# An LSTM with a feed-forward network: the input products of the last 24 steps as seven products of quarters, and the gates in two pairs

## The chip, the core and the metric

The kernel runs on one core of a Trainium2 chip. The time is that of one launch on the device, in microseconds (us). PE is the matrix engine, ACT the scalar engine, DVE the vector engine, POOL the general-purpose engine, SP the engine that only issues transfers (DMAs). Each engine takes its instructions in program order and waits on semaphores for the others. The time before is 312.69 us, the median of three runs (312.64 to 312.83).

## What is computed

```python
def lstm_forward(x, h0, Wx, Wh, b):            # x (32, 64, 256), h0 = cond (32, 256)
    xW = jnp.einsum('ntd,dg->ntg', x, Wx) + b  # g: 4 * 256 columns, gates i, f, o, g
    def step(carry, xw_t):
        a = xw_t + prev_h @ Wh
        i, f, o = sigmoid of the first three gates of a;  g = tanh of the fourth
        next_c = f * prev_c + i * g
        next_h = o * jnp.tanh(next_c)
...
h = s0 * dense(k0, concatenate([h, -h]));  h = relu(h) * 2    # weights are +1 or -1 by bool
h = s1 * dense(k1, h);  h = relu(h) * 2                       # 1024 x 1024
h = s2 * dense(k2, h)
out = x + h
```

There are 64 dependent steps on a batch of 32, then three dense layers over all 2048 rows.

## The kernel before

**Layout.** A gate of 256 columns is spread over four groups of 32 partitions (q = 0 to 3), so that one step's batch of 32 fills 128 partitions with 64 columns for each gate. A product with 32 columns of stationary operand uses a quarter of the array's columns, and the kernel issues four of them side by side, one for each q. Such four matmuls are called a pass here. `x_part` (line 242) makes one pass of x Wx for a step `t` and half `k` of the 256 inputs: all four gates (256 moving columns), or two gates (128 columns), which is half a pass. A matmul of f32 stands in the trace as two instructions.

**Recurrence.** `gates_from_h` (line 301) adds h Wh to two PSUM banks: the first bank holds the gates g, i, f (192 columns), the second o (64 columns); the order in memory is `GATES = (3, 0, 1, 2)`. `cell_step` (line 319) applies on ACT sigmoid to i and f, tanh to g, sigmoid to o; DVE makes `kept`, `new` and `c`; ACT makes `th` = tanh(c); DVE makes `h` and turns it into `hist`, the next stationary operand. Last, ACT copies x Wx + b of the next step into the two gate banks (`gates_from_x`, lines 316 and 317).

**Order.** The order is written out by hand: each engine runs what the main loop (line 702) emits, in that order. A step emits the gates and the cell first, then filler work for PE, then chores for DVE and ACT. In the first `X_STEPS` = 21 steps the filler is x Wx of later steps (`x_products`, line 272); in the other 43 it is the dense layers of blocks of 16 steps (`ffn_block`, line 585), 576 matmuls of 512 columns in all. The filler is dealt out evenly by a running `goal`: 208 half passes over 21 steps are nine or ten for each step. The last block of 16 steps follows after the loop (`last_block`).

**Chores in the first stretch.** DVE adds the bias to each full bank of x Wx (`evict_x`, line 258, two steps' worth of 512 columns), turns blocks of x (`turn_x`, line 226, by `next_x`, which also issues the load of x two blocks on, on SP), makes parts of the weights `w0` (line 206) and the low half of h (`split_h`, line 344: ACT rounds `hist` to `hhi`, DVE forms the rest `hlo`; the dense layers read both). ACT also makes `w0t` (line 205) and one 1024-column row of `w1` in a step (line 211). A counter `load` of DVE chores in the step holds further chores back from two on; a split that has waited long enough is emitted in any case.

**Start.** PE first runs two matmuls that clear the gate banks and eight idle ones (`WARM_UP`). Wx arrives in six transfers, issued by SP and ACT. The products of the first eight steps are made in three sweeps: input half 0 with the slots 1 and 2, input half 0 with the slots 0 and 3, then input half 1 with all gates. Between the last two come the bias products. POOL issues the small transfers, makes some single-column constants, and then has nothing to do.

Of the kernel before, what the change touches and what calls it, by code (L numbers as in the profile page):

```python
# [30 lines left out]
F32 = mybir.dt.float32  # L33
# [8 lines left out]
def lstm_ffn(ctx: ExitStack, tc: tile.TileContext, x, cond, wx_d, wh_d, b_d, k0_d, k1_d, k2_d, s0_d, s1_d, s2_d, out):  # L42
    nc = tc.nc
# [13 lines left out]

    GATES = (3, 0, 1, 2)

    AHEAD = 12  # L60
    X_STEPS = 21

    FIRST_CHORE = 2
    W2_STEP = 24
    WARM_UP = 8

# [15 lines left out]
    def act(shape, dtype, name):  # L82
        return apool.tile(shape, dtype, tag="act", name=name)
# [33 lines left out]

    def load_gates(t, w_d, slots, engines, chunks=slice(0, 2)):

        w_rows = w_d.rearrange("(p b) g -> p b g", b=2)  # L120
        s0, n, g0 = slots[0], len(slots), GATES[slots[0]]
        if len(engines) == 1:
            halves = [slice(0, P)]
        else:
            halves = [slice(0, P // 2), slice(P // 2, P)]
        for engine, half in zip(engines, halves):
            engine.dma_start(
                out=t[half, chunks, s0 * H : (s0 + n) * H], in_=w_rows[half, chunks, g0 * H : (g0 + n) * H]
            )


    both = [nc.sync, nc.scalar]
    load_x(0, 0, both)
    for k in range(2):
        load_gates(wx, wx_d, (1, 2), [nc.sync], slice(k, k + 1))
        for slot in (0, 3):
            load_gates(wx, wx_d, (slot,), [nc.scalar], slice(k, k + 1))
    load_x(0, 1, both)
    load_gates(wh, wh_d, (1, 2), both)
    load_gates(wh, wh_d, (0,), [nc.scalar])  # L140
    load_gates(wh, wh_d, (3,), [nc.sync])

# [3 lines left out]
    b_rows = b_d.rearrange("(o g h) -> o g h", o=1, g=4)  # L146
    nc.gpsimd.dma_start(out=b_row[0][:1, :1], in_=b_rows[:, 3:])
    nc.gpsimd.dma_start(out=b_row[0][:1, 1:], in_=b_rows[:, :1])
    nc.gpsimd.dma_start(out=b_row[1][:1], in_=b_rows[:, 1:3])
    scales = []  # L150
# [58 lines left out]

    def make_w1(k):  # L210
        nc.scalar.activation(w1[:, k, :], bits[k], AF.Identity, bias=nsgn[1], scale=sgn2[1])  # L211
        load_bits(4 + k)

# [22 lines left out]

    load = [0]

# [19 lines left out]
    def evict_x(p, t):  # L258
        xg[t] = gpool.tile([P, 2, 4 * HQ], F32, tag="xg", name=f"xg{t}")
        b = bias.rearrange("p g j -> p (g j)").unsqueeze(1).to_broadcast([P, 2, 4 * HQ])  # L260
        load[0] += 1
        nc.vector.tensor_tensor(xg[t], p.rearrange("p t g j -> p t (g j)"), b, ALU.add)  # L262

    def next_x(half):

        if half < 2 * NB:
            load[0] += 1
            turn_x(*divmod(half, 2))
            if half + 4 < 2 * NB:
                load_x(*divmod(half + 4, 2), [nc.sync])  # L270

    def x_products(t0, t1):

        for t in range(t0, t1, 2):
            p = x_bank(t)
            for s in range(2):
                for k in range(2):
                    start = s == 0 and k == 0
                    passes = min(left_over[0], 2)
                    if passes == 1:  # L280
                        x_part(p, t + s, k, slice(0, 2), start)
                        yield 1
                        x_part(p, t + s, k, slice(2, 4), False)
                    else:
                        x_part(p, t + s, k, slice(0, 4), start)
                    if s == 1 and k == 1:
                        evict_x(p, t)
                        half, left = divmod(t + 2, SB // 2)
                        if left == 2 and half + 1 < 2 * NB:
                            turns.append(half + 1)  # L290
                        if left == 6 and turns:
                            next_x(turns.popleft())
                    yield passes


    hist, hparts = {}, {}

    gate_banks = [ps_g.tile([P, TB], F32, tag=f"gates{n}", name=f"gates{n}") for n in (3, 1)]
    gates = [g[:, : n * HQ].rearrange("p (g j) -> p g j", j=HQ) for g, n in zip(gate_banks, (3, 1))]

    def gates_from_h(t, hT):
        for g, slots in zip(gates, (slice(0, 3), slice(3, 4))):
            for k in range(2):
                for q in range(NQ):
                    nc.tensor.matmul(  # L305
                        g[q * N : (q + 1) * N],
                        hT[:, k, :],
                        wh_q[:, k, q, slots],
                        start=False,
                        stop=(k == 1),  # L310
                        skip_group_check=True,
                    )

    def gates_from_x(t):
        x_t = xg[t // 2 * 2][:, t % 2].rearrange("p (g j) -> p g j", g=4)
        nc.scalar.copy(gates[0], x_t[:, :3])  # L316
        nc.scalar.copy(gates[1], x_t[:, 3:])  # L317

    def cell_step(t, c):
        sig = cell.tile([P, 3, HQ], F32, tag="sig", name=f"sig{t}")  # L320
        cand = cell.tile([P, HQ], F32, tag="cand", name=f"cand{t}")
        nc.scalar.activation(sig[:, 0:2, :], gates[0][:, 1:3], AF.Sigmoid)  # L322
        nc.scalar.activation(cand, gates[0][:, 0], AF.Tanh)  # L323
        nc.scalar.activation(sig[:, 2, :], gates[1][:, 0], AF.Sigmoid)  # L324
# [33 lines left out]
    def evict(p, name):  # L358
        hi, lo = (act([P, TB], F32R, f"{name}{s}") for s in "hl")
        load[0] += 1  # L360
        nc.scalar.activation(hi, p, AF.Relu)
        nc.vector.scalar_tensor_tensor(lo, p, 0.0, hi, ALU.max, ALU.subtract)  # L362
        return hi, lo
# [276 lines left out]
    for g in gate_banks:  # L640
        nc.tensor.matmul(g, idle[:, :P], idle, start=True, stop=True)  # L641
    for n in range(WARM_UP):
        nc.tensor.matmul(p_idle, idle[:, :P], idle, start=True, stop=True)  # L643
# [10 lines left out]
    def copy_bias():  # L654
        p_bias = ps_o.tile([P, 4, HQ], F32, tag="po", name="p_bias")
        for q in range(NQ):
            for i, t in enumerate(b_row):
                nc.tensor.matmul(  # L658
                    p_bias[q * N : (q + 1) * N, 2 * i : 2 * i + 2],
                    first,  # L660
                    t.rearrange("p g (q j) -> p q g j", q=NQ)[:, q],
                    start=(i == 0),
                    stop=True,
                    skip_group_check=True,
                )
        nc.vector.tensor_copy(bias, p_bias)

    banks = [x_bank(t) for t in range(0, SB // 2, 2)]
    for slots in (slice(1, 3), slice(0, 4, 3)):
        for t in range(SB // 2):  # L670
            x_part(banks[t // 2], t, 0, slots, t % 2 == 0 and slots.start == 1)
    copy_bias()
    for t in range(SB // 2):
        x_part(banks[t // 2], t, 1, slice(0, 4), False)
        if t % 2:
            evict_x(banks[t // 2], t - 1)
            if t == 1:
                turn_x(0, 1)
# [13 lines left out]
    chores += [lambda k=k, h=h: make_w0(k, h) for k in range(2) for h in range(2)]  # L692
    chores += [lambda k=k: make_w1(k) for k in range(FC0)]
    chores2 = deque(lambda k=k, m=m: make_w2(k, m) for k in range(2) for m in range(2))
    sum_parts = deque(lambda s=s, k=k: make_sum(s, k) for k in range(K2) for s in range(1, 5))
    splits, w0_parts = deque(), deque()

    work = x_products(AHEAD, T)
    total_x = (T - AHEAD) * 4
    total_ffn = (NB - 1) * (4 * FC0 + 2 * FC0 * FC1 + 4 * FC1)  # L700
    done = 0
    for t in range(T):
        load[0] = 0
        gates_from_h(t, hT)
# [3 lines left out]
        if outputs:  # L708
            load[0] += 1
            if next(outputs[0], "end") == "end":  # L710
                outputs.popleft()
        if t == X_STEPS:
            work, done = ffn(), 0
        goal = (t + 1) * total_x // X_STEPS if t < X_STEPS else (t + 1 - X_STEPS) * total_ffn // (T - X_STEPS)
        while done < goal:
            left_over[0] = goal - done
            done += next(work)
        if t == X_STEPS - 1:
            next(work, None)

        if turns and load[0] < 2:
            next_x(turns.popleft())
        if splits and (load[0] < 2 or t >= X_STEPS or t == SH * splits[0] + 2 * SH - 1):
            split_h(splits.popleft())
        else:
            if t >= FIRST_CHORE and chores:
                part = chores.popleft()()
                if part is not None:
                    w0_parts.append(part)
            elif t >= W2_STEP and chores2:  # L730
                chores2.popleft()()
            if w0_parts and (load[0] < 2 or t == X_STEPS - 1):
                w0_parts.popleft()()
            if sum_parts and t >= SUM_STEP and load[0] < 2:
                sum_parts.popleft()()
    assert not sum_parts
# [31 lines left out]
```

## Time and profile before

| what | value |
|---|---|
| median of three runs | 312.69 us |
| the profiled execution, its own time | 312.31 us |
| its span, first to last instruction | 310.5 us |
| start, to the first gates | 16.60 us |
| first stretch, 21 steps | 63.4 us, a step mostly 3.03 us |
| second stretch, 43 steps | 183.4 us, a step 4.18 or 4.41 us |
| after the loop | 47.1 us |
| busy in the first stretch, of 63.40 us | PE 63.40, DVE 45.62, ACT 37.71, POOL 0.00 us |
| busy in the second, of 183.40 us | PE 183.28, DVE 96.51, ACT 80.70, POOL 0.00 us |
| granted PE clock | 1.00 in all stretches of the loop |

The last rows come from a table of busy time by stretch. A matmul's busy time runs until its result is written, so matmuls overlap in it, and a busy PE is not yet one at its peak; start-to-start times tell more. Busy time on the other engines is plain.

### The profile page before, as it was taken

The numbers are of one execution on the slowest core, as the hardware profiler recorded it, in microseconds if no ns is written. First come the engines' busy times: TensorE is split into PE (matmuls) and PEld (weight loads), VectorE is DVE, ScalarE is ACT, GpSimd is POOL, SyncE is SP. The second block draws the span as 40 slices with busy tenths as digits, with TensorE's granted clock in tenths as the row PEclk, the third lists the DMA queues.
The fourth block names the chain that finished last, engine by engine and source line by source line (L and its number), as shares of the span: only waits on it lengthen the run. The fifth ranks groups of instructions, "written<-read, shape, count | busy, mean of one in ns | idle before, by whom it ended". The sixth has DMA issues, their size and how long they took to land.

```text
span 310.5 us, 9798 instructions
## 1 busy us (share of the span) xinstructions
PE 304.5 (98%) x4138; PEld 242.7 (78%) x4138; DVE 178.1 (57%) x530; ACT 142.0 (46%) x512; POOL 6.6 (2%) x24
## 2 busy tenths in 40 slices
PE   8999999999999999999999999999999999999994
PEld 4888888788777777777777777777777777899993
DVE  2566767777673444355754445567554434698543
ACT  0225566774564543435633434355443333886220
POOL 5300000000000000000000000000000000000000
PEclk9999999999999999999999999999999999999999
DMA  6874001142000000000010000000310000131002
GB/s 192 206 196 99 5 19 38 36 95 65 3 2 0 2 2 0 3 2 0 2 38 22 14 3 0 2 2 13 92 34 2 3 0 2 31 79 27 2 0 69
DMA packets 30587, 10.89 MB, mean 35 GB/s; under 512 B 27720, under 2 KB 29768, under 8 KB 30544
## 3 DMA queue, kind: packets, MB, share of 16 engines
q1 hardware_dynamic: 27136, 8.66, 11.2%
q10 hardware_dynamic: 3168, 1.57, 2.0%
q8 instruction: 32, 0.52, 0.7%
q0 software_dynamic: 240, 0.04, 0.1%
q14 instruction: 11, 0.09, 0.1%
HBM read 8.16 MB, written 2.10 MB: 33 GB/s over the span
## 4 chain that ended last, share of the span: by engine, by line
PE 97%; DVE 1%; ACT 0%; issue 0%; ACTq 0%
PE p L617 30%; PE gates L305 20%; PE px L246 18%; PE p L591 8%; PE po L604 7%; PE gates L452 4%; PE po L561 2%; PE r L452 2%; PE x L452 2%; PE p L479 2%; PE p_idle L643 1%; PE gates L641 0%; DVE a_7l L362 0%; DVE o L388 0%; PE p_bias L658 0%
## 5 line engine op out<-in xcount | busy, mean ns | idle before, releaser
L305 PEld LDWEIGHTS gates<-wh,hist 128*32 128x32 f32 x2016 | 54.6, 109 | 22.3 <-issue 13.4
L305 PE MATMUL gates<-wh,hist 128*32 128x192 f32 x2016 | 68.1, 275 | 0.0
L246 PE MATMUL px<-wx,xT 128*32 128x256 f32 (+1 forms) x1168 | 60.5, 353 | 0.1
L322 ACT ACTIVATE sig<-gates 128x128 f32<-128x128 f32 x64 | 17.7, 277 | 80.6 <-PE gates L305 80.4
L246 PEld LDWEIGHTS px<-wx,xT 128*32 128x32 f32 x1168 | 42.4, 110 | 11.3 <-DVE c_first L652 0.7
L326 DVE TENSOR_TENSOR kept<-sig,c 128x64 f32<-128x64 f32 x63 | 14.2, 225 | 50.0 <-ACT sig L322 49.7
L332 ACT ACTIVATE th<-c 128x64 f32<-128x64 f32 x64 | 16.4, 257 | 31.4 <-DVE c L330 31.4
L334 DVE TENSOR_TENSOR h<-sig,th 128x64 f32<-128x64 f32 x64 | 14.4, 225 | 20.7 <-ACT th L332 20.7
L262 DVE TENSOR_TENSOR xg<-px,bias 128x512 f32<-128x512 f32 x32 | 21.2, 671 | 2.8 <-PE px L246 2.3
L316 ACT COPY gates<-xg 128x192 f32<-128x192 f32 x64 | 20.0, 313 | 1.3 <-DVE xg L262 1.3
L591 PE MATMUL p<-hhi,w 128*128 128x512 f32 x48 | 19.3, 402 | 0.0
L591 PE MATMUL p<-hlo,w 128*128 128x512 f32 x48 | 19.1, 398 | 0.0
L339 DVE STREAM_TRANSPOSE hist<-h 128x64 f32<-128x64 f32 x64 | 15.7, 245 | 2.4
L330 DVE TENSOR_TENSOR c<-kept,new 128x64 f32<-128x64 f32 x64 | 14.4, 224 | 2.2
L324 ACT ACTIVATE sig<-gates 128x64 f32<-128x64 f32 x64 | 14.9, 233 | 0.1
L323 ACT ACTIVATE cand<-gates 128x64 f32<-128x64 f32 x64 | 14.0, 218 | 0.0
L328 DVE TENSOR_TENSOR new<-sig,cand 128x64 f32<-128x64 f32 x64 | 13.9, 217 | 0.0
L317 ACT COPY gates<-xg 128x64 f32<-128x64 f32 x64 | 13.0, 203 | 0.0
L591 PEld LDWEIGHTS p<-hhi,w 128*128 128x128 f32 x48 | 9.0, 188 | 2.2
L591 PEld LDWEIGHTS p<-hlo,w 128*128 128x128 f32 x48 | 9.0, 188 | 2.0
L211 ACT ACTIVATE w<-bits,nsgn,sgn 128x1024 fp32r<-128x1024 uint8 x8 | 9.9, 1241 | 0.0
L617 PE MATMUL p<-a_7h,w 128*128 128x512 f32 x24 | 9.9, 413 | 0.0
(249 smaller groups left out, 602.8 us busy)
## 6 DMA issues: line engine op xcount, KB each, us to landing
x<-in_x_dram SPq DMA_DIRECT2D x60, 64.0 KB, 2.8
out_dram<-o SPq DMA_DIRECT2D x28, 64.0 KB, 1.8
bits<-in_L_ffn_k_dram SPq DMA_DIRECT2D x10, 128.0 KB, 3.2
wx<-in_L_cond_Wx_dram SPq DMA_DIRECT2D x2, 256.0 KB, 4.2
wx<-in_L_cond_Wx_dram ACTq DMA_DIRECT2D x4, 128.0 KB, 4.6
wh<-in_L_cond_Wh_dram ACTq DMA_DIRECT2D x2, 256.0 KB, 5.6
wh<-in_L_cond_Wh_dram SPq DMA_DIRECT2D x2, 256.0 KB, 6.2
k<-in_L_ffn_k_dram SPq DMA_DIRECT2D x2, 256.0 KB, 3.1
```

The source lines that it names most:

```text
L246: nc.tensor.matmul(p[q * N : (q + 1) * N, t % 2, slots], xT[i // 2, i % 2][:, s, k, :], wx_q[:, k, q, slots], start=start, stop=False, ski ...
L262: nc.vector.tensor_tensor(xg[t], p.rearrange("p t g j -> p t (g j)"), b, ALU.add)
L305: nc.tensor.matmul(g[q * N : (q + 1) * N], hT[:, k, :], wh_q[:, k, q, slots], start=False, stop=(k == 1), skip_group_check=True,)
L316: nc.scalar.copy(gates[0], x_t[:, :3])
L322: nc.scalar.activation(sig[:, 0:2, :], gates[0][:, 1:3], AF.Sigmoid)
L324: nc.scalar.activation(sig[:, 2, :], gates[1][:, 0], AF.Sigmoid)
L332: nc.scalar.activation(th, c, AF.Tanh)
L339: nc.vector.transpose(hT, h.rearrange("p (j b) -> p b j", b=2))
L452: nc.tensor.matmul(bank[pair][:, i], a(k)[:, ts(2 * pair + i, P)], b(k, n), start=first and i == 0 and k == 0 and n == 0, stop=last and k ...
L591: nc.tensor.matmul(p, w0[:, k, ts(m, P)], a[:, k, :], start=(n == 0), stop=(n == 3))
L604: nc.tensor.matmul(po[m], w2[:, m, k], a1[k][n], start=(k == 0 and n == 0), stop=(k == FC1 - 1 and n == 1))
L617: nc.tensor.matmul(p1[m], w1[:, k, ts(m, P)], a0[k][n], start=(k == 0 and n == 0), stop=(k == FC0 - 1 and n == 1),)
```

## The change

The x Wx of the steps 40 to 63 (eight-step halves of blocks, numbers 5, 6 and 7) is no longer made step by step. For each such half the product is a 2 x 2 block product: the inputs in two halves, the steps in two groups of four, the gates in two pairs (i, f) and (o, g). Instead of eight block products seven are made, on sums and differences: four sums of blocks of Wx on POOL (`sum_wx`, once), four differences of blocks of x on DVE for each half (`differ_x`), and copies and sums of the results by ACT and DVE. Each of the seven has four half passes. The gates stand in memory as i, f, o, g, the two gate banks hold a pair each (128 columns each), Wx arrives in five transfers and in another order, and the bias in two. `make_w1` makes half a row at a time; chores of ACT are counted in `copies`, those of DVE in columns (`load`, up to `ROOM`). Two of the idle matmuls now clear two banks for the quarters. The first stretch has 20 steps.

```diff
-    X_STEPS = 21
+    X_STEPS = 20
+    TURN_STEPS = (5, 9, 13)
+    BEGIN_STEPS = (8, 12, 15)
+    FIRST_QUARTERS = 5
+    QUARTERS = [
+        [(5, 1), (5, 7)], [(5, 2), (5, 6)], [(5, 5), (6, 1)], [(5, 3), (5, 4)], [(6, 7), (6, 6)], [(6, 2), (6, 5)],
+        [(7, 1), (6, 3)], [(6, 4), (7, 7)], [(7, 6), (7, 2)], [(7, 5)], [(7, 3), (7, 4)],
+    ]
-    WARM_UP = 8
+    WARM_UP = 6
...
+    for gates, k, engine in (
+        (slice(0, 2), 0, nc.sync), (slice(2, 3), 0, nc.scalar), (slice(3, 4), 0, nc.sync),
+        (slice(0, 2), 1, nc.scalar), (slice(2, 4), 1, nc.sync),
+    ):
+        load_gates(wx, wx_d, gates, [engine], slice(k, k + 1))
...
+    def sum_wx():
+        a11, a12 = wx[:, 0, : 2 * H], wx[:, 1, : 2 * H]
+        a21, a22 = wx[:, 0, 2 * H :], wx[:, 1, 2 * H :]
+        for i in (1, 2, 3, 4):
+            t = wx_sum[i] = act([P, 2 * H], F32, f"sx{i}")
...
+            nc.gpsimd.tensor_tensor(t, in0, in1, op)
+    def differ_x(i, ns):
...
+        load[0] += 360
+        for n in ns:
+            in0, in1 = {1: (b12, b11), 2: (b22, t[:, 0]), 3: (b22, b12), 4: (b21, t[:, 1])}[n]
+            nc.vector.tensor_tensor(t[:, n - 1], in0, in1, ALU.subtract)
+    def take_x(i, pair, half, p, other):
...
+        load[0] += 512
+        nc.vector.tensor_tensor(flat(t), flat(p), other, ALU.add)
+    def begin_r(i):
+        r = quarter_bank(ps_f, "pf", f"qr{i}")
...
+        nc.scalar.copy(flat(r), bias_of(1))
+    def x_products_of(i, n):
...
+        p = {1: x, 2: x, 7: r, 4: r}.get(n, q)
+        for s in range(SB // 4):
+            for k in range(NQ):
+                nc.tensor.matmul(
+                    p[k * N : (k + 1) * N, s],
+                    b[:, s],
+                    w[:, k],
...
+        if n == 1:
+            q = banks["q"] = quarter_bank(ps_o, "po", f"qq{i}")
...
+            nc.scalar.copy(q, x)
+        elif n == 2:
+            take_x(i, 0, 0, x, bias_of(0))
+        elif n in (6, 5):
+            t = uv[i, n] = act([P, SB // 4, 2, HQ], F32, f"uv{i}_{n}")
...
+            nc.scalar.copy(t, q)
+            if n == 5:
+                take_x(i, 1, 1, r, flat(t))
+        elif n == 3:
+            take_x(i, 0, 1, q, bias_of(0))
+        elif n == 4:
+            take_x(i, 1, 0, r, flat(uv[i, 6]))
...
-        nc.scalar.activation(sig[:, 0:2, :], gates[0][:, 1:3], AF.Sigmoid)
-        nc.scalar.activation(cand, gates[0][:, 0], AF.Tanh)
+        nc.scalar.activation(sig[:, 0:2, :], gates[0], AF.Sigmoid)
+        nc.scalar.activation(cand, gates[1][:, 1], AF.Tanh)
         nc.scalar.activation(sig[:, 2, :], gates[1][:, 0], AF.Sigmoid)
...
+        if t in TURN_STEPS:
+            turns.append(FIRST_QUARTERS + TURN_STEPS.index(t))
+        if t in BEGIN_STEPS:
+            begin_r(FIRST_QUARTERS + BEGIN_STEPS.index(t))
+        if X_STEPS - len(QUARTERS) <= t < X_STEPS:
+            for i, n in QUARTERS[t - X_STEPS + len(QUARTERS)]:
+                x_products_of(i, n)
+                done += 4
...
+        if differences:
+            differ_x(*differences.popleft())
-        if turns and load[0] < 2:
+        if turns and (load[0] + 512 <= ROOM or turns[0] >= FIRST_QUARTERS):
             next_x(turns.popleft())
+        if w0_parts and load[0] + 512 <= ROOM:
+            load[0] += 512
+            w0_parts.popleft()()
-        if splits and (load[0] < 2 or t >= X_STEPS or t == SH * splits[0] + 2 * SH - 1):
+        if splits and (load[0] + 320 <= ROOM or t >= X_STEPS or t == SH * splits[0] + 2 * SH - 1):
             split_h(splits.popleft())
+            load[0] += 320
+            copies[0] += 1
+        while t >= FIRST_CHORE and chores and copies[0] < 2:
```

## The prediction, made before the change was run

> **What bounds the kernel.** I read the page's chain of waits first, then the same chain in order of time, then one step's timeline.
>
> ```profile
> PE 97%; DVE 1%; ACT 0%; issue 0%; ACTq 0%
> ```
>
> All but 3% of the span is PE following PE. In order of time, for steps 9 to 11:
>
> ```profile
> 44.00 0.87 PE gates L305 x32
> 44.87 2.16 PE px L246 x48
> 47.03 0.87 PE gates L305 x32
> 47.91 1.95 PE px L246 x40
> 49.85 0.93 PE gates L305 x32
> 50.78 2.16 PE px L246 x40
> ```
>
> A step of the first stretch is gates (0.87 us) and filler (ten half passes, 2.16 us). With nine it should shrink by 0.216 us. The step from 46.82 to 49.70 has nine and shrank from 3.03 to 2.88 only: there the recurrence was the limit. Its timeline (start, length, what; brackets: idle before):
>
> ```profile
> 46.82 1.08 PE L305 MATMUL gates<-wh,hist 128*32 128x192 f32 x32
> ...
> 47.80 0.28 ACT L322 ACTIVATE sig<-gates 128x128 f32<-128x128 f32 x1 [0.28 <-PE gates L305]
> 47.98 0.22 ACT L323 ACTIVATE cand<-gates 128x64 f32<-128x64 f32 x1
> ...
> 48.25 0.22 DVE L328 TENSOR_TENSOR new<-sig,cand 128x64 f32<-128x64 f32 x1
> ...
> 49.31 0.24 DVE L339 STREAM_TRANSPOSE hist<-h 128x64 f32<-128x64 f32 x1
> ...
> 49.67 0.95 PEld L305 LDWEIGHTS gates<-wh,hist 128*32 128x32 f32 x32 [0.30 <-ACT gates L317]
> 49.70 1.08 PE L305 MATMUL gates<-wh,hist 128*32 128x192 f32 x32
> ```
>
> The last wait is put down to a copy that ended at 49.38; it was hist, ending at 49.55. So the recurrence alone takes 2.88 us, 0.15 less than a full step: little room. In the second stretch a step is 4.18 us (13 matmuls) or 4.41 (14), so it has over 1 us of room, and only PE's work counts. One of its matmuls is 0.2265 us, hence a step's gates there, with the change of form, cost 4.18 - 13 x 0.2265 = 1.24 us. Check: 43 x 1.24 + 576 x 0.2265 = 183.8, measured 183.4.
>
> **Fewer products, shorter ones.** Three halves of eight steps took 32 half passes each and take 28: 12 fewer. But they are all of 128 columns. Busy time by stretch, of two sweeps at the start (64 instructions, eight half passes each):
>
> ```profile
> 5.44:7.22 1.78, 1.78 (x65) 1.68 (x64) 0.00 (x0) 0.00 (x0) 0.00 (x0) 1.00 0.95 293
> 7.51:9.26 1.75, 1.75 (x64) 1.75 (x65) 0.00 (x0) 0.53 (x1) 0.72 (x4) 1.00 0.67 167
> ```
>
> 1.75 / 8 = 0.218 us a half pass, against 0.216 in the 256-column form. A rule speaks against the change here: the Trainium skill, "TensorEngine Tiling (Array Packing)", Instruction Overhead, gives every matmul about 60 cycles of overhead. Four matmuls side by side start as one group, two groups to a pass of either width; so 84 half passes are 168 groups where 42 full passes had 84. Taken as an addition [...]the rule asks 84 x 25 ns = 2.1 us, most of the gain. The rows give 2 x 109.2 - 215.9 = 2.5 ns, 0.2 us in all; I take them, since they are this shape. The gates' 192 + 64 columns become 128 + 128: the same columns, 0.87, no change.
>
> PE's own sum for 20 steps is then 16 of 3.04 (ten half passes) and 4 of 2.82 (nine: steps 0, 5, 10, 15; 196 half passes over 20): 59.9 us, against 63.4 for 21. **Minus 3.5.** The gates of the step that leaves move to the second stretch: **plus 1.24**. Its 576 matmuls are unchanged.
>
> **The pairs lengthen the recurrence.** sig came 0.98 us after the gates began, 0.33 after the 0.65 of its bank's four groups. cand now waits for both banks: 0.87 + 0.33 = 1.20, where it was 1.16 (47.98 - 46.82). sig (i, f) comes earlier, at 0.77, but new needs cand. I take +0.05 (bounds 0 and +0.1): 2.93 us. Steps of nine now cost 2.93 instead of 2.82: 4 x 0.12 = **plus 0.5**.
>
> **DVE chores beyond their room.** In a step they start 2.71 us after the gates began (hist at 2.54, then 0.17, as from 49.31 to 49.48) and must leave DVE by 1.34 us into the next step, or new is late: 1.67 us in a step of 3.04. Start-to-start times of before: xg 0.60 (0.57 to 0.64), turned x 0.69, hlo 0.34 (0.33 to 0.40), w0 part 0.67 to 0.73. A difference of 128 columns is not in the trace; between 64 columns (0.22) and 256 (0.40) I take 0.29; the second pair (2, 4) is dependent, 0.51 for both, the first 0.40 (bounds 0.3 and 0.7). The order of the changed program then overloads these steps:
> - Step 7: xg, turned x (which issues no load any more), differences, hlo: 0.60 + 0.69 + 0.51 + 0.34 = 2.14, 0.48 over. Step 8 takes 2.93 + 0.48 = 3.41: plus 0.38.
> - Step 11: ACT copies the quarter's sum first (2.64 to 3.23), so DVE's sum starts at 3.26; with differences and hlo it ends at 4.71, 0.33 over: step 12 plus 0.23.
> - Step 14: the copy waits for the second product (2.95 to 3.54), sum and differences end at 4.57, 0.19 over; step 15, one of nine, plus 0.19.
>
> Together **plus 0.8** (bounds 0 and 1.5). The other quarter steps fit: ACT's copies (512 columns, 0.59 as the evictions) and half rows of w1 (0.72, as w0t) end by 4.06, and sig may start at 4.1. The turns issue no other transfers than before, and SP's later queue is untouched.
>
> **The dense layers begin one step after the last split.** Before, hlo of step 19 came long ahead of the first dense product at 81.03:
>
> ```profile
> 76.44 0.24 DVE L339 STREAM_TRANSPOSE hist<-h 128x64 f32<-128x64 f32 x1
> 76.61 0.65 DVE L262 TENSOR_TENSOR xg<-px,bias 128x512 f32<-128x512 f32 x1
> 77.18 0.40 DVE L355 TENSOR_TENSOR hlo<-hist,hhi 128x256 fp32r<-128x256 f32 x1
> ```
>
> Step 20 was the cover. Now the dense layers start in step 20, and in step 19 two quarter sums and an xg stand ahead of hlo: 2.71 + 3 x 0.6 + 0.4 = 4.9 us after step 19's gates, PE's second dense matmul wants it at 3.04 + 1.35 = 4.39. With 0.12 from DVE to PE and 0.05 of lateness, PE stands still 0.7 us, with all later work behind it: **plus 0.7** (0.4 to 0.9).
>
> **The start.** PE waits 0.29 us at 7.22 for slot 3 of input half 0. When it landed the trace tells by an issue: transfers raise eight semaphores in turn, and SP's issue of wh that reuses this one goes out at 7.40. The new order puts that piece second on SP, behind 256 KB; the transfer that stood second there had landed by 7.16, when ACT's issue of wh that waited for it went out. I take **minus 0.25** (-0.29 to +0.5, the latter if it shares its time with the 256 KB now second on ACT). Ten clearing and idle matmuls remain ten.
>
> **POOL's sums** are free where they end before step 0. POOL is idle from 11.4 us, and no row has a wide POOL operation. The Trainium skill, "GPSIMD Engine Reference", Performance versus the Vector engine, prices 2048 columns of two inputs at 4.50 us and advises DVE instead[...]. A quarter each is an estimate of 4.5 us, ending near 16, before DVE's first such operation (17.91) and far ahead of their first use at 43.8. On DVE they would cost 4 x 0.67 = 2.7 us, also in room. I take 0 (0 to +0.5, if step 0 is slowed).
>
> **Sum** in the profiled execution: -3.5 + 1.24 + 0.5 + 0.8 + 0.7 - 0.25 = -0.5 (-0.55 unrounded), so 312.31 becomes 311.8 and the span 310.0. The median of the runs stands 0.38 above the profiled execution: 312.1. Most of what is saved is spent on lateness elsewhere.
>
> **Rivals.**
> - The lateness does not appear (chores shorter, chain as before): -3.5 + 1.24 - 0.25 = -2.5, or half way, -1.5: medians of 310.2 to 311.2. For it: DVE was busy only 72% of the first stretch; against: the order above. 0.27.
> - Slower: the recurrence becomes the limit of every first-stretch step. Place: cand behind bank 2. Only 0.10 us is left in a full step; beyond it each 0.01 costs 16 full, four short and three late steps. At 0.15 more than I take: 16 x 0.05 + 7 x 0.15 = 1.9, giving 314.0; slower by 0.2% from 0.12. For it: 2.88 of 3.03 used; against: it takes three times the delay that the row shows. 0.13.
> - The transfers' order costs instead: +0.5 for -0.25, 312.9. 0.10.
> - The quarters wait for POOL or a bank, so the change does not do what it says: near 313. 0.05.
> - My forecast, own range 311.7 to 312.6: 0.45.
>
> 0.2% is about what a measurement of this kernel tells from no change: 0.63 us, faster below 312.06, slower above 313.3. The forecast lies just at the first line; of its 0.45 I give 0.17 to faster. Faster 0.27 + 0.17 = 0.44; slower 0.13; the same 0.43. The range: 310.8 leaves out the clean case's lower half, 313.1 most of the slower one.
>
> **What would show it.** Steps of 2.93 at 0, 5, 10; a step near 3.4 at 8; PE idle 0.7 us before a dense product on hlo; no gap near 7.2; half passes of quarters at 0.218. Wrong if steps are 3.04 throughout, or if PE waits on cand's chain in full steps.

## The result, and the profile after

**Slower, by about half a per cent.** The changed kernel takes 314.22 us (median of 16 runs, 312.56 to 316.26), the kernel before 312.67 us in the same comparison (16 runs, 312.42 to 313.03): a ratio of 1.0048, 95% interval 1.0032 to 1.0064. The forecast was 312.1 us, with a range of 310.8 to 313.1. Two things stand out: the time went up where a small gain was summed, and the runs lie 3.7 us apart where those of before lie 0.6 us apart.

The profiled execution took 314.74 us, its span 312.9 us. The chain of waits on its page, by engine:

```profile
PE 94%; DVE 2%; DMA 1%; issue 1%; ACT 1%; SPq 0%; ACTq 0%
```

PE was 97% of the chain before; now 6% of the span is not PE following PE. Busy time of the first stretch, before (first columns: stretch, its length, PE busy):

```profile
16.60:80.02 63.42, 63.42 (x1591) 51.99 (x1585) 45.64 (x146) 37.71 (x143) 0.00 (x0) 1.00 0.27 66
```

and after:

```profile
17.48:80.27 62.79, 61.76 (x1845) 54.57 (x1837) 46.80 (x150) 45.07 (x156) 0.00 (x0) 1.00 0.24 59
```

Twenty steps take 62.79 us, where the sum asked for 61.2, and PE has idle time, 1.03 us, where it had none. It also runs more instructions in fewer steps, 1845 matmuls (and about as many weight loads) for 1591. The chain in order of time shows where PE stands (step 13: start, length, what):

```profile
57.20 1.06 PE gates L417 x32
58.26 0.87 PE qr L377 x32
59.13 0.87 PE qq L377 x32
60.01 0.06 PE px L253
60.07 0.53 issue
60.59 0.53 PE px L253 x12
```

A quarter costs 0.87 us, four half passes of 0.218, as summed. But after one matmul of `px` PE does nothing for 0.53 us, and the row names no semaphore: "issue" is waiting for nothing that the profile shows. The twelve matmuls behind it belong to the same product, with the same operands, into the same bank. From start to start the gap is 0.80 us, of which a matmul is 0.02 to 0.03. A second gap of 0.50 us comes at 64.02 and a third of 0.53 us at 68.03, the third in the middle of the gates' matmuls.

Counted over PE's instructions from the start of the trace (weight loads, matmuls and the semaphore and drain instructions of its sequencer), the three gaps stand behind numbers 3009, 3265 and 3521. **They are exactly 256 apart.** The view of transfers shows what comes in pieces of 256 instructions. Its queue rows for 50 to 75 us, before:

```profile
q8 instruction: 5, 0.08, 1.3%
```

and after:

```profile
q8 instruction: 7, 0.11, 1.9%
```

The columns are packets, MB and share of the DMA engines. Queue 8 carries PE's own program, 16 KB in a packet (0.11 MB in 7). The Trainium skill, "Runtime: NRT & Kernel Launch", Instruction fetch mechanics, says the same of its size: blocks of 16 KiB or 256 instructions, the next fetched while the current one runs. It calls the cost of a new block mostly hidden. Here it is not. Read from the single packets and instructions of the trace, from 47 to 80 us:

```
                              before        after
PE time of 256 instructions   4.5 to 5.7    3.5 (steps of two quarters)
packet ends ahead of the
 first instruction of the
 block by                     3.0 to 4.5    1.3 to 1.5
next packet starts after        3.9 to 5.9    3.4 to 4.8
 the last one by
starved blocks begin          60.59, 64.52, 68.56: 3.93 and 4.04 apart
```

Before, a block lay ready for 3 us and more; after, PE takes up each block 1.3 to 1.5 us after its packet ended. In none of the 17 traces of this case does it take one up earlier than 1.2 us after, so a block is here no sooner ready than PE needs it, and three times it is late. Blocks of 3.5 us leave no time in hand. The gates of a step are 64 instructions, a full pass of x products is 16, a quarter 64: a step of before has 144, one of two quarters 208 to 224.

Could other transfers have held the packets up? The data queue's rows for the same 50 to 75 us, before and after:

```profile
q1 hardware_dynamic: 5696, 1.57, 26.7%
```

```profile
q1 hardware_dynamic: 3232, 0.79, 14.2%
```

Before moved twice as much there, without a gap. And the packet ahead of the longest gap, from 58.08 to 59.06 us, is the only packet of any queue between 57.5 and 61.5 us:

```profile
DMA packets 1, 0.02 MB, mean 4 GB/s; under 512 B 0, under 2 KB 0, under 8 KB 0
```

So the gaps need no other traffic.

### The profile page after: what moved, and what is told of

It reads as the page before. It is cut to its first block, busy times and chain, and to the rows that moved or that the text cites. A ratio compares the mean times of both kernels' runs of the same rounds, so it can differ in the third digit from the quotient of the medians.

```text
span 312.9 us, 10415 instructions
## 1 busy us (share of the span) xinstructions
PE 305.1 (98%) x4426; PEld 247.2 (79%) x4426; DVE 184.6 (59%) x542; ACT 155.6 (50%) x532; POOL 11.1 (4%) x27
## 4 chain that ended last, share of the span: by engine, by line
PE 94%; DVE 2%; DMA 1%; issue 1%; ACT 1%; SPq 0%; ACTq 0%
PE p L733 30%; PE gates L417 20%; PE px L253 11%; PE p L707 7%; PE po L720 7%; PE gates L568 4%; PE po L677 2%; PE r L568 2%; PE x L568 2%; PE qq L377 2%; PE p L595 2%; PE qx L377 2%; PE qr L377 1%; DMA wx<-in_L_cond_Wx_dram 1%; DVE xq L348 0%
## 5 line engine op out<-in xcount | busy, mean ns | idle before, releaser
L417 PE MATMUL gates<-wh,hist 128*32 128x128 f32 x2016 | 69.1, 275 | 0.5 <-issue 0.3
L417 PEld LDWEIGHTS gates<-wh,hist 128*32 128x32 f32 x2016 | 53.4, 109 | 18.4 <-issue 13.8
L253 PE MATMUL px<-wx,xT 128*32 128x256 f32 (+1 forms) x784 | 40.9, 344 | 0.9 <-issue 0.5
L253 PEld LDWEIGHTS px<-wx,xT 128*32 128x32 f32 x784 | 29.1, 112 | 7.6 <-DVE c_first L772 1.2
L433 ACT COPY gates<-xg 128x128 f32<-128x128 f32 x80 | 18.1, 258 | 3.7 <-DVE xg L269 3.7
L269 DVE TENSOR_TENSOR xg<-px,bias 128x512 f32<-128x512 f32 x20 | 13.2, 670 | 3.6 <-PE px L253 3.4
L440 ACT ACTIVATE sig<-gates 128x64 f32<-128x64 f32 x64 | 14.0, 219 | 0.1
L215 ACT ACTIVATE w<-bits,nsgn,sgn 128x512 fp32r<-128x512 uint8 x16 | 12.6, 810 | 0.0
L433 ACT COPY gates<-xq 128x128 f32<-128x128 f32 x48 | 10.9, 258 | 0.0
L733 PE MATMUL p<-a_6l,w 128*128 128x512 f32 x24 | 9.7, 404 | 0.0
```

The costliest lines, as they stand in the source:

```text
L253: nc.tensor.matmul(p[q * N : (q + 1) * N, t % 2, slots], xT[i // 2, i % 2][:, s, k, :], wx_q[:, k, q, slots], start=start, stop=False, ski ...
L417: nc.tensor.matmul(g[q * N : (q + 1) * N], hT[:, k, :], wh_q[:, k, q, ts(i, 2)], start=False, stop=(k == 1), skip_group_check=True,)
L433: nc.scalar.copy(g, x_t)
L733: nc.tensor.matmul(p1[m], w1[:, k, ts(m, P)], a0[k][n], start=(k == 0 and n == 0), stop=(k == FC0 - 1 and n == 1),)
```

## The experiments

**Theory A**: PE runs out of fetched instructions wherever 256 of them are worked off in less than about 4 us. **Theory B**: what the prediction already held, lateness of DVE and of the chain through `cand`, only larger. Medians are given with the ratio to the kernel before on the same chip and its 95% interval. The table at the end of this section has all parts.

**Half passes in the kernel before (two runs).** Its filler is put out in half passes: the same columns, no quarter, no sums, twice the instructions. In all steps (half_all), or for the products of steps 40 to 63 (half_late):

```
-                    passes = min(left_over[0], 2)
+                    passes = 1 if t0 >= AHEAD else min(left_over[0], 2)   # half_all
+                    passes = 1 if t >= 40 else min(left_over[0], 2)       # half_late
```

> The kernel before, with all filler products of the first stretch cut into half passes of 128 columns: the same columns for PE, twice the PE instructions in the filler (224 a step instead of 144). Theory A (PE's instructions arrive in blocks of 256, and a block takes about 4.0 us to come): 256 instructions last 3.47 us at PE's speed, so PE stands still some 0.5 us every 256 instructions; 18.4 blocks, 21 steps in about 73 us instead of 63.4, 321 to 323 us. Theory B (lateness on DVE and ACT and the landing of Wx alone, no limit on instructions): 208 half passes at 2.5 ns, 313 us.

> The kernel before, with only the products of steps 40 to 63 in half passes of 128 columns (96 half passes, no quarters). Theory A: about ten steps at 224 PE instructions, eight or nine blocks each about 0.5 us late: 316 to 317 us, and a wider spread of the runs. Theory B: 312.9 us.

Measured: half_all 318.91 us, 1.0211 (1.0195 to 1.0227); half_late 314.95 us, 1.0075 (1.0055 to 1.0095). Groups of half_all's page, and of before's (the last column is PE's idle time ahead of that group):

```profile
L246 PE MATMUL px<-wx,xT 128*32 128x128 f32 (+1 forms) x1920 | 65.0, 282 | 3.7 <-issue 3.5
```

```profile
L246 PE MATMUL px<-wx,xT 128*32 128x256 f32 (+1 forms) x1168 | 60.5, 353 | 0.1
```

and one gap of half_all in its timeline:

```profile
67.07 0.83 PE L246 MATMUL px<-wx,xT 128*32 128x128 f32 x23
...
68.59 0.86 PE L246 MATMUL px<-wx,xT 128*32 128x128 f32 x24 [0.68 <-issue]
```

PE, which never stood in the first stretch of before, now waits 3.5 us for nothing shown, again inside one run of like matmuls. Start to start, ten gaps of 0.2 to 1.1 us add up to 6.05 us; its stretch from step 1 on is 6.68 us longer. All ten have instruction numbers (961, 1217, 3009 and so on to 5057) that leave 193 when divided by 256. This is the change's loss without the change: B has nothing to offer, and A alone foresaw slower kernels, by more than came (321 to 323 us for half_all, 316 to 317 for half_late).

**The change without its quarters.** No turned or summed x: X_STEPS 21, all halves in full passes; the new gates, the new order of Wx and POOL's sums stay.

```
-    X_STEPS = 20
+    X_STEPS = 21
-    FIRST_QUARTERS = 5
+    FIRST_QUARTERS = 8
...
+    QUARTERS = []
```

> The changed kernel without quarters (all steps by full passes, 21 steps; the gates in pairs, the new order of Wx and the sums on POOL stay). Theory A with the start's loss apart: steps of ten half passes 3.03, of nine 2.92, no stall inside a run of matmuls; first gates near 17.4 us as in the changed kernel; 313.3 to 313.7 us. If the runs spread as little as those of before, the spread comes from the quarters' instructions; if they spread over 3 us, from the transfers at the start.

Measured: 312.69 us (312.14 to 313.54), 1.0009 (1.0001 to 1.0017). No gap at any block; steps of nine half passes take 2.926 and 2.914 us (2.895 and 2.880 before), so pairs of gates lengthen the recurrence by 0.03. The median lies 0.6 us below what was expected, because the start's loss did not come: step 1 begins at 19.17 us. All of the loss but 0.1% goes with the quarters.

**The order of Wx (two runs).**

```
-    for gates, k, engine in (
-        (slice(0, 2), 0, nc.sync), (slice(2, 3), 0, nc.scalar), (slice(3, 4), 0, nc.sync),
-        (slice(0, 2), 1, nc.scalar), (slice(2, 4), 1, nc.sync),
-    ):
-        load_gates(wx, wx_d, gates, [engine], slice(k, k + 1))
+    for k in range(2):
+        load_gates(wx, wx_d, slice(0, 2), [nc.sync], slice(k, k + 1))
+        for gate in (2, 3):
+            load_gates(wx, wx_d, slice(gate, gate + 1), [nc.scalar], slice(k, k + 1))
```

> The changed kernel with Wx cut and ordered over SP and ACT as before (the first pair on SP, single gates on ACT). If the new order delays the start, the first product begins at 5.44 us again and the first gates at 16.3 to 16.6 us instead of 17.48: about 0.9 us less, 313.2 to 313.4 us at the median. If the start is set by something else (the bias, POOL), no change: 314.2 us.

> The changed kernel with Wx cut and ordered as before, a second time on another day's chip. If the new order of Wx really costs time, the ratio is again 1.001, 0.2 to 0.3% below the changed kernel's 1.0032 to 1.0048. If that difference came from the instruction blocks falling differently, 1.003 to 1.005 as the changed kernel.

Measured: 312.83 us, 1.0012 (1.0002 to 1.0023), then 313.38 us, 1.0029 (1.0016 to 1.0041). The first product began at 5.97 us in wx_order, not at 5.44, so neither of its two expectations came true. Its median alone would have put 0.2 to 0.3% on the new order; the second takes that back, being level with the changed kernel's own second measurement (1.0032, below). Step 1 begins at 19.84 and 20.56 us with the old order, at 20.39 and 21.00 with the new, at 19.17 without quarters and with the new order: the start scatters by more than the order could be worth, and no effect of it is shown.

**64 instructions more ahead of everything.**

```
-    for n in range(WARM_UP):
+    for n in range(WARM_UP - 3):
         nc.tensor.matmul(p_idle, idle[:, :P], idle, start=True, stop=True)
+    for n in range(35):
+        nc.tensor.matmul(p_idle[:, :16], idle[:, :P], idle[:, :16], start=True, stop=True)
```

> The changed kernel with three of the six long idle matmuls of the start replaced by 35 short ones: 64 PE instructions more, all of them before the first product, and nothing else different. Theory A (PE runs out of fetched instructions): the standstills inside runs of matmuls stay 256 instructions apart and at the same remainder of the instruction number, so they fall 64 instructions earlier in the program than in the changed kernel: not at instructions 3009, 3265 and 3521 of the changed kernel's count but at 2945, 3201, 3457 (about 0.9 us earlier, in front of other matmuls), 0.2 to 0.9 us each. Rival (a place of the program is to blame: a bank, a late operand, a collision with a chore of steps 13, 14 and 16): they stay in front of the same matmuls. The time itself tells nothing here: 312.5 to 316 under both.

Measured: 313.44 us, one run. The gaps of the first stretch did not move, they were missing, and so they were in another execution of the changed kernel itself; this run says little about those. A single gap was left, of 0.50 us in the start, behind its own instruction 449. The changed kernel's next execution has its gap of the start behind 449 too, which is 64 instructions later in the program. So that gap kept to the number.

**The changed kernel once more**, unchanged.

> The changed kernel itself, a second time, so that the edits can be compared on one chip and its standstills can be seen in a second profiled execution. Theory A (PE runs out of fetched instructions, by a margin that differs from run to run): again 313.5 to 314.8 with a spread of over 1.5 us; standstills inside runs of matmuls again only where the instruction number leaves 193 when divided by 256, but not all of the same ones as in the first execution. Rival (a fixed lateness of the program): the same steps are late by the same times in both executions.

Measured: 313.83 us (312.48 to 314.87, 22 runs), 1.0032 (1.0020 to 1.0044). Steps 13 and 14, in its chain in order of time:

```profile
57.77 1.08 PE gates L417 x32
58.85 0.87 PE qr L377 x32
59.72 0.87 PE qq L377 x32
60.59 0.44 PE px L253 x16
61.03 0.87 PE gates L417 x32
```

The `px` that stood for 0.80 us runs through. Steps 13, 14 and 16 take 3.05, 3.06 and 3.12 us, where the first execution had 3.77, 3.58 and 3.53. Its only gaps at block ends are 0.64 us at 449 and 0.36 us at 4289. Here the packets of the blocks begun between 49.6 and 63.8 us ended 2.0 to 2.5 us ahead of their block, and blocks of 3.46 to 3.7 us were just kept up with. So the supply is near its limit, and which side of it a run falls on differs from run to run: that is the likely source of the wider scatter, with the start's. A fixed lateness of the program is ruled out, since the program is the same.

**The last split early.** The prediction's standstill on `hlo` is in the profile of after, in its timeline:

```profile
81.51 0.50 PE L707 MATMUL p<-hhi,w 128*128 128x512 f32 x1
...
81.82 0.40 DVE L471 TENSOR_TENSOR hlo<-hist,hhi 128x256 fp32r<-128x256 f32 x1
...
82.28 0.50 PE L707 MATMUL p<-hlo,w 128*128 128x512 f32 x1 [0.27 <-DVE hlo L471]
```

The first dense product starts at 81.51, the second, which needs `hlo`, at 82.28: 0.77 us from start to start. The same pair before, with no wait:

```profile
81.03 0.50 PE L591 MATMUL p<-hhi,w 128*128 128x512 f32 x1
81.37 0.40 PE L591 MATMUL p<-hlo,w 128*128 128x512 f32 x1
```

That is 0.34 us, so the wait on `hlo` itself is 0.43 us; the 0.77 that the next text gives to the standstill is the whole distance. It goes if the split is made in step 16 (split_16), here also with the old order of Wx (wx_split):

```
-        if splits and (load[0] + 320 <= ROOM or t >= X_STEPS or t == SH * splits[0] + 2 * SH - 1):
+        if splits and (load[0] + 320 <= ROOM or t >= X_STEPS or t == SH * splits[0] + 2 * SH - 1 or t == X_STEPS - 4):
```

> The changed kernel with the last split of the first block (hlo) forced into step 16, so that it no longer stands behind the sums of step 19. Prediction's step 'the dense layers begin one step after the last split': the standstill of 0.77 us ahead of the second dense product goes, step 20 takes 4.18 to 4.25 us instead of 4.95, and the kernel gains 0.7 (0.4 to 0.8) against the changed one; step 17 may be late by up to 0.3. Theory A leaves the standstills at every 256th instruction as they are: median 313.0 to 313.8, still above the kernel before. Rival (PE would only wait for the next thing, the gates of step 20): gain below 0.2.

> The changed kernel with Wx cut and ordered as before and the last split of the first block in step 16. If the new order of Wx costs time at the start (as the two medians so far suggest: 312.83 with the old order, 314.22 with the new) and the standstill on hlo costs 0.7, the two add up: 311.8 to 312.4. If the order is worth nothing and that difference came from the instruction blocks, this is as split_16: 312.3 to 312.8.

Measured: 312.53 us (312.19 to 313.86), 1.0002 (0.9992 to 1.0012), and 312.83 us (311.69 to 314.26), 1.0003 (0.9990 to 1.0016). No wait on `hlo` is left in step 20; in split_16 the step took 4.56 us, 0.24 of it a gap at number 4289, where 4.18 to 4.25 was expected. The gain against the changed kernel, about 0.3% or 1 us, is more than the 0.7 expected, but the intervals leave room for 0.7, and the profiled execution of split_16 also had few gaps at blocks. wx_split is at the edge of what was expected if the order is worth nothing. Both kernels are level with before. wx_split's fastest run is 1.0 us under the median before; in its profiled one, of 314.26 us, four blocks cost 2.46 us between steps 13 and 20.

**The quarters spread thinly (six runs).** Quarters over 15 or 16 steps instead of 11 make 176 instructions the usual step and 208 the exception. Each run has its own list; from spread_split on, the split of step 16 is in. The first and the last:

```
-    TURN_STEPS = (5, 9, 13)
-    BEGIN_STEPS = (8, 12, 15)
...
+    TURN_STEPS = (3, 6, 12)      # spread, spread_split
+    BEGIN_STEPS = (4, 10, 15)
+        [(5, 1)], [(5, 7)], [(5, 2)], [(5, 6)], [(5, 5), (6, 1)], [(5, 3)], [(5, 4)], [(6, 7), (6, 2)],
+        [(6, 6)], [(6, 5)], [(6, 3), (7, 1)], [(6, 4)], [(7, 7), (7, 2)], [(7, 6)], [(7, 5)], [(7, 3), (7, 4)],
...
+    TURN_STEPS = (3, 9, 11)      # spread6
+    BEGIN_STEPS = (2, 9, 17)
+        [(5, 1)], [(5, 6)], [(5, 7)], [(5, 2), (5, 5)], [], [(5, 4), (6, 1)], [(6, 6)], [(6, 7), (6, 5)],
+        [(6, 2)], [(5, 3), (7, 1)], [(6, 3)], [(7, 2), (6, 4)], [(7, 6)], [(7, 7), (7, 5)], [(7, 3), (7, 4)],
```

(The quarters are 21; the next text counts them as 22.)

> The changed kernel with its 22 quarter products spread over 16 steps (4 to 19), one or two a step, instead of two a step over 11: about 184 PE instructions in a step where the changed kernel has up to 224, so that 256 instructions last 4.2 us instead of 3.5. PE's work is the same. Theory A (a block of 256 instructions takes about 4 us to come): most of the standstills inside runs of matmuls go (1.83 us in the profiled execution of the changed kernel at 59.8, 64.0 and 68.0); gain 1.0 to 1.8 us against the changed kernel, median 312.3 to 313.2, and runs that lie closer together than its 312.6 to 316.3. Rival B (the prediction's: lateness of DVE and the chain through cand): the chores fall on other steps and nothing is gained in sum: 314 to 315.

> Both edits at once: quarters spread over 16 steps and the last split of the first block in step 16. Theory A with the prediction's term of 0.7: the gains add up, 1.7 to 2.5 us against the changed kernel, median 311.6 to 312.5, below the kernel before or level with it. If B were right: 313.3 to 314.3.

> The changed kernel with its 21 quarter products over steps 4 to 19 in another order than in spread, so that the banks of two halves are not held at once while a filler product needs one, and with the last split in step 16. Theory A: no step has two quarters next to another with two, a block of 256 instructions lasts 4 us or more nearly everywhere, standstills at block ends below 0.5 us in sum; steps 12 to 16 take 2.93 to 3.2; no standstill on a bank in step 10; median 311.3 to 312.3, below the kernel before. Rival B (lateness of DVE's chores decides, wherever they stand): 312.8 to 313.8.

> As spread2 with a third order of the quarters (step 8 without one, the last half's started later). Theory A: as spread2 within 0.4 us, 311.3 to 312.4. Rival B: 312.8 to 313.8.

> The changed kernel with its 21 quarter products over steps 5 to 19 in a fourth order (turns in steps 3, 8, 12), chosen so that no product asks for a turned x, a difference or a bank before it is there (what spread, spread2 and spread3 lost 1.4, 1.2 and 0.4 us by), and with the last split in step 16. Theory A: no standstill over 0.2 us on a bank or an operand in the first stretch, blocks cost 0.3 to 0.9 us in sum, step 9 at most 3.3: median 311.4 to 312.2, faster than the kernel before by 0.5 to 1.2 us. If blocks of 256 instructions come too late even at 176 instructions a step, or the start loses more than the steps gain: 312.5 to 313.2.

> As spread5 with a fifth order (turns in steps 3, 9, 11; no quarter in step 9, so three doubled steps lie nearer together). Theory A: DVE is late nowhere by over 0.1 us, blocks cost 0.1 to 0.4 more than in spread5: 311.4 to 312.3. Otherwise 312.5 to 313.2.

Measured: spread 313.89 us, 1.0035 (1.0023 to 1.0047); spread_split 313.74, 1.0035 (1.0022 to 1.0047); spread2 313.68, 1.0030 (1.0018 to 1.0043); spread3 313.25, 1.0025 (1.0012 to 1.0037); spread5 313.37, 1.0027 (1.0009 to 1.0045); spread6 312.63 (311.80 to 313.81), 1.0003 (0.9993 to 1.0014). None reached what theory A expected of it; spread6 is level with before, the others are slower. In spread, gaps at blocks fell from 1.77 to 0.58 us, but a wait of its own took their place (timeline, step 10):

```profile
49.61 0.64 PE L253 MATMUL px<-wx,xT 128*32 128x256 f32 x8
...
50.56 0.65 DVE L348 TENSOR_TENSOR xq<-qr,uv 128x512 f32<-128x512 f32 x1
...
51.27 0.86 PE L253 MATMUL px<-wx,xT 128*32 128x256 f32 x16 [1.01 <-DVE xq L348]
```

Two halves hold banks at once, and the filler has to wait until DVE has emptied one: 1.39 us from start to start. spread2 asks in step 9 for an x that is just being turned:

```profile
45.85 0.70 DVE L248 STREAM_TRANSPOSE xT<-x 128x512 f32<-128x512 f32 x1
...
46.70 1.08 PE L391 MATMUL qx<-wx,xT 128*32 128x128 f32 x32 [0.65 <-DVE kept L456]
```

The row names `kept`, but that ended at 46.65 and the product does not read it; the turn, which ended at 46.55, is what it reads. spread6 avoids both, and its stretch has a single gap at a block end, in step 14:

```profile
62.38 0.27 PE L266 MATMUL px<-wx,xT 128*32 128x128 f32 x1
...
63.34 0.53 PE L266 MATMUL px<-wx,xT 128*32 128x128 f32 x12 [0.68 <-issue]
```

This is number 3265 again, 0.93 us. Spreading thins the gaps out but does not end them: steps of 208 and 176 instructions in turn, as its steps 10 to 14 are, can still be too dense. That spread_split, spread2 and spread3 came out where rival B put them says that my lists were late on their own account, on banks and operands; it does not bring B back for the changed kernel, which has none of these waits. No version beat the kernel before; the best, spread6 and split_16, are level with it.

All profiled executions, cut at the start of step 1 and of the first step with dense products. Blocks: sum of the gaps of 0.2 us or more, from start to start and less the ordinary 0.02, at numbers that leave 193 when divided by 256, from 6 to 85 us.

```
               to step 1  first stretch  rest     blocks
before           19.50       60.52      230.51    none
after            20.39       59.88      232.61    1.77
after_again      21.00       58.34      232.67    1.00
no_quarters      19.17       60.55      230.64    none
wx_order         19.84       59.76      232.58    2.04
wx_order_again   20.56       58.67      232.67    1.21
shift_64         20.82       58.21      232.55    0.50
split_16         19.78       58.43      232.20    0.48
wx_split         20.15       59.90      232.43    2.46
spread           19.91       60.00      232.24    0.58
spread_split     19.38       60.05      232.44    0.84
spread2          20.25       59.76      232.29    0.58
spread3          21.36       59.84      231.97    1.83
spread5          20.36       58.61      232.54    0.88
spread6          20.19       58.69      232.00    0.93
half_all         20.27       67.20      230.64    6.05
half_late        19.51       62.93      231.11    2.45
```

(The first stretch has 21 steps in before, no_quarters and the two of half passes, 20 elsewhere, so the rest has one step less there.)

## Why the prediction was wrong

**The step that failed is PE's own sum for 20 steps, 16 of 3.04 and 4 of 2.82.** It takes PE's time as work alone and puts the wait for instructions at nothing; in the profiled execution that wait was 1.77 us in three gaps. The half pass of 0.218 us came from two sweeps of the start. Each sweep has 64 matmuls and so 128 instructions, half a block, and both (5.44 to 9.26 us) ran before the first packet on queue 8 had landed, at 9.58 us: such a stretch can't show what many blocks in a row cost. The sum counted columns and steps, not instructions, so a limit on their supply had no place in it, nor had any rival one. The bound on the recurrence, the slower rival, didn't come about: steps of nine half passes took 2.92 to 2.99. That its 314.0 us lies next to the measured 314.22 is chance.

What the rest of the sum is worth shows in the execution with no block gap over 0.2 us between steps 1 and 20, after_again. Its first stretch from step 1 on is 58.34 us; summed were 61.2 less a step 0 of 2.93, 58.3. In the first execution it is 59.88: 1.54 more, against 1.77 us of gaps at 3009, 3265 and 3521. So the gaps cover all that was missing there. That 58.34 meets 58.3 so closely is in part luck: the chores made steps 8, 12 and 15 late by 0.6 of the 0.8 us taken, and step 19 was late by 0.16, which was not foreseen.

**Point by point.**
- Quarters at 0.218 us a half pass: right (0.87 for four). The rule of 25 ns for each matmul, which was weighed and not taken, finds no more support here than in the trace of before: 0.87 us for the four is what the rows gave without it.
- Gates in pairs: 2.93 us for a step of nine; measured 2.915, 2.994 and 2.921 in steps 0, 5 and 10.
- Chores beyond their room: step 8 at 3.41, measured 3.27; step 12 late by 0.23, measured 3.30, 0.26 over 3.04; step 15 late, measured 2.93, not late. In sum 0.5 of the 0.8 taken in this execution.
- `hlo`: 0.7. The second dense product came 2.01 us after the step's gates began, where it was wanted at 1.35: 0.66 us late, of which 0.43 is the wait for `hlo`. The rest of the kernel, with the gates of the step that moved, was to grow by 1.94 and grew by 2.10. In spread6, with neither that wait nor a gap in step 20, it grew by 1.49. So the step that moved seems to cost nearer 1.5 than 1.24 and `hlo` nearer 0.6 than 0.7: the sum is right in part because two errors offset.
- The start: -0.25, measured +0.89 to step 1 in the first execution and +1.50 in the second, of which 0.64 is a block. The expected gap at 7.2 is gone, but the first product waits for its Wx:

```profile
6.05 0.65 PE L253 MATMUL px<-wx,xT 128*32 128x128 f32 x8 [0.36 <-DMA wx<-in_L_cond_Wx_dram]
```

It began at 5.44 us before and begins at 6.05. Over all kernels it lies between 5.27 and 6.22, with either order. The reading took one landing in one trace for a fixed time. Why the landing scatters is open, and so is how much of the start's loss comes with the change; the runs don't separate it from the blocks.
- POOL's sums: 1.28 us each, ending at 17.1 us, and step 0 took 2.915: free, as taken.

With the gaps of the stretch and the error of the start taken off, the profiled execution would be 314.74 - 1.77 - 1.14 = 311.8 us, the number predicted for it. So the miss is mainly two terms, a missing one and a mis-sized one; that the rest meets to 0.1 us is luck in part, as said above. That the gaps at blocks are a limit of supply is shown by their numbers in 15 kernels and executions that have any, by the packets and by the half passes. In the trace of after a block's coming has three parts: from PE's entry into the block before to the start of the packet, the packet itself (0.9 to 1.5 us), and from its end to PE's entry (1.3 to 1.5 us). Ahead of the three gaps the first part was 1.7 to 2.0 us, in the five blocks around them 1.0 to 1.3 (1.9 at number 4289, which came 0.1 us late). So it was the start of the packet that was late; what made it late was not found.

## What to carry to other kernels

Count PE's instructions as well as its columns: cutting the columns by an eighth gained nothing here, because each cut product takes as many instructions as a full one of twice the width, and where 256 instructions lasted about 4 us or less, PE had to wait for its program at some of the blocks. A gap "issue" inside a run of like matmuls, at instruction numbers a multiple of 256 apart, is the mark of it, and runs that scatter more than before can be its shadow. A duration measured over half a block says nothing of the rate at which many follow.

## What was not expected of the hardware

- PE's program comes on a DMA queue of its own in packets of 16 KB (35 of them in the page of after, 0.57 MB), each 0.9 to 1.5 us long, and PE takes up a block no earlier than 1.2 us after its packet ended (the least of 17 traces, in split_16; 1.3 in after). Starved blocks followed one another after 3.6 to 4.5 us (half_all), 3.93 and 4.04 in after.
- The margin is thin, and 4 us is no threshold. Before, at 4.5 to 5.9 us a block, no gap was seen; but gaps came also after blocks of 4.1 us (spread_split and spread3 at number 1473, 0.41 and 0.69 us), of 4.3 us (wx_split at 4289, 0.43 us) and in the start of 5.4 us (after_again at 449, 0.64 us). There the packet began 3.2 us after PE had entered the block before, where in before it began 0.7 us after.
- POOL's sum of two 128x512 operands took 1.28 us, 5.1 for the four where 4.5 was estimated.
